# The counted groups' products in fp32 instead of three bf16 parts, with the counts widened on ScalarE

## The chip, the core and the metric

The kernel runs on one core of one Trainium2 chip. The metric is the device time of one execution in microseconds. A core has five engines with instruction streams of their own: TensorE (PE, with its weight loads as PEld), VectorE (DVE), ScalarE (ACT), GpSimd (POOL) and SyncE (SP). They wait for each other by semaphores. SP's stream here holds nothing but DMA issues; POOL's holds the gathers.

## The reference

Two layers of a graph network, a last product, and a normalized residual, on 12500 nodes of 256 features with 200000 edges sorted by `dst`:

```python
def _sage_conv(x, src, dst, W_l, b_l, W_r):
    msgs = x[src]
    agg = jax.ops.segment_sum(msgs, dst, num_segments=N_NODES)
    deg = jax.ops.segment_sum(jnp.ones((src.shape[0],), x.dtype), dst, num_segments=N_NODES)
    mean = agg / jnp.maximum(deg, 1.0)[:, None]
    return mean @ W_l + b_l + x @ W_r
h = relu(_sage_conv(x, src, dst, W1_l, b1, W1_r))
h = relu(_sage_conv(h, src, dst, W2_l, b2, W2_r))
out = layernorm(x + h @ W3 + b3)
```

`dst` is 12500 times the square of a uniform number, so low nodes have many edges and high nodes few. Everything is fp32.

## The kernel before

Nodes are handled in 98 blocks of 128, edges in 1563 tiles of 128. A node's sum over its edges is formed in one of two ways.

**Counted groups.** The hot nodes, those with many edges, come in groups of 256. For a group, `count` (L724) builds a matrix of counts, how often each source row occurs for each of the group's nodes: for every tile of edges DVE makes one-hot tables `pick`, `low` and `aft` (L738 to L746), PE multiplies them into `count_ps` (L765, L776, L780), and ACT writes the result to `counts` in bf16 (L782). `product` (L681) then multiplies the whole table of rows by the counts: for each of the 98 blocks of rows, PE accumulates rows times counts in PSUM (`dense_ps`, L707). So that these products are exact in bf16, the fp32 rows are split beforehand in three bf16 parts whose sum they are (`exact`, L656): those of `x` in the first stage (`split_rows`, L668, stored in `x3_d`), those of `h` when each block of the first layer is done (L976, stored in `h3_d`). A block of rows takes 3 parts x 2 halves of the features, six products of 128x256. Layer 1 counts five groups. Layer 2 uses eight: four whose counts layer 1 has stored in `count_d` and that are streamed back (`beside`, with sums in `beside_ps`) and four that are counted or kept; each of its four stages makes products for two groups at once, twelve for a block of rows. `degrees` (L791) sums a group's counts by 980 products of one column in all, to have the nodes' degrees on the partitions (`rdeg`).

**Gathers.** The edges of the other nodes are gathered: a round is four indirect DMAs of 128 rows from POOL into one of four buffers `got` (L262), then PE sums the rows by a one-hot `one` that DVE makes two rounds ahead (L274, four strips of 32 columns), ACT copies the result (`some`, L284), and one step later PE spreads it over the nodes (L290) and DVE adds it to `sums`, a ring of 8 blocks (L304). Layer 1 has 269 rounds, layer 2 has 235. A gather into a buffer waits until PE has summed what was in it.

**Blocks.** When all edges of a block are summed, `first_block` (L954) or `last_block` (L980) makes its output: rows are loaded and transposed on PE (L902), copied by ACT (L904), multiplied by both weights (`sage`: L925 for the sums, L930 for the own rows), combined on DVE (L936, L937) with the reciprocal degree as a scale for each partition, and passed through relu on ACT (L939). The last block transposes its result `h` once more, multiplies by `W3` (L997) and normalizes. A block is a generator; each `yield` ends a piece.

**The order.** The orders of PE and POOL are those in which the program is written (`manual_schedule`, L459). `layer` (L602) goes through the rounds and cuts each in three turns. In a turn it runs at most one piece of at most two open blocks (`MOST`), a block's next piece being due two turns after the last (`APART`), and fills up with counting and dense products: `mixed` (L815) interleaves a stage's parts in proportion to costs that the code states (`COST_DENSE` 0.7 for six products, `COST_DEGREES`, `count_cost`), and each round gets an equal share of the layer's sum of costs. In the third turn the sums of the round before (`summed`) come ahead of the piece. The loads of rows go through SP in the order of the program; four buffers of two blocks each hold them (`NROWS`, L692).

Of the kernel before, what the change touches and what calls it, by code (L numbers as in the profile page):

```python
# [23 lines left out]
P = 128  # L24
# [23 lines left out]
def by_runs(  # L48
# [82 lines left out]
    x3_d = dram.tile([P, NB, 3, D], BF16, name="x3_d")  # L131
    h3_d = dram.tile([P, NB, 3, D], BF16, name="h3_d")
# [8 lines left out]
    place = consts.tile([1, len(groups)], I32, name="place")  # L141
# [7 lines left out]
    offs = [consts.tile([1, n], I32, name=f"offs{g}") for g, n in enumerate(tiles_of)]  # L149
# [34 lines left out]
    rdeg = early.tile([P, NB], F32, name="rdeg")  # L184

    part_pool = ctx.enter_context(tc.tile_pool(name="part_ps", bufs=1, space=PSUM))
    mixed_pool = ctx.enter_context(tc.tile_pool(name="mixed_ps", bufs=2, space=PSUM))
# [3 lines left out]
    NROWS = 4  # L191
# [42 lines left out]
    class Gathers:  # L234
# [20 lines left out]
        def gathered(self, i):  # L255
# [13 lines left out]
            if r == 0:  # L269
                self.part_ps = part_pool.tile([P, D + 1], F32, name="part_ps")  # L270
            part_ps, width = self.part_ps, self.width

            for j in reversed(range(G)):
                strip = nc.tensor.matmul(part_ps[j * W:(j + 1) * W, :width], lhsT=one[:, j],  # L274
# [9 lines left out]
            nc.scalar.copy(some[:, :width], part_ps[:, :width])  # L284
# [289 lines left out]
    biases = consts.tile([P, 3, D], F32, name="biases")  # L574
    for i, b in enumerate((b1, b2, b3)):
        nc.scalar.dma_start(biases[:, i], b[None, :].to_broadcast([P, D]))
    zero = consts.tile([P, 1], F32, name="zero")
# [8 lines left out]
    split = keep.tile([P, 2, 3, D], BF16, name="split")  # L586
# [13 lines left out]
    MOST, APART = 2, 2  # L600

    def layer(gathers, block, n_pieces, dense, dense_cost, left):  # L602
# [5 lines left out]
        def begin():  # L608
            if waiting and len(queue) < MOST:
                b, *of = waiting.pop(0)  # L610
                p = block(b, *of)
                next(p)
                queue.append([b, p, n_pieces - 1, turn + APART])

        def pieces():
# [5 lines left out]
            if q:  # L621
                next(q[1])
                q[2:] = q[2] - 1, turn + APART
                if q[2] == 0:
                    done.add(q[0])
                    queue.remove(q)
# [12 lines left out]
        for i in range(i0, n + 1):  # L639
# [3 lines left out]
            for part in range(3):  # L643
                if part == 2 and before:
# [4 lines left out]
                pieces()  # L649
# [6 lines left out]
    def exact(t, s, rest):  # L656


        def upper(a):
            return a.bitcast(BF16).rearrange("p (n h) -> p n h", h=2)[:, :, 1]  # L660
# [5 lines left out]
        return leaves  # L666

    def split_rows(b):  # L668
        t = load_rows(x, N, b, "split_sb")
        s = split[:, b % 2]  # L670
        leaves = exact(t, s, work.tile([P, D], F32, name="rest", tag="own"))
        if b < 3:
            later(leaves)
        nc.sync.dma_start(x3_d[:, b], s)

# [5 lines left out]
    def product(table3, g, c_sb, beside=None):  # L681
# [6 lines left out]
        for t in ps:  # L688
            nc.tensor.matmul(t, lhsT=zeros_b, rhs=c_sb[:, :NC, :DN], start=True, stop=False)
        for b in range(NB):  # L690
            if b % 2 == 0:
                rows = work.tile([P, 2, 3, D], BF16, name="rows", bufs=NROWS)  # L692
                loads = [(nc.sync.dma_start(rows, table3[:, b:b + 2]), NROWS)]
                if beside is not None:
                    stream = streams[n_streamed % STREAMS]
                    n_streamed += 1
# [702 lines left out]
```

## Time and profile before

| what | value |
|---|---|
| three runs | 3265.1, 3281.22 (median), 3290.72 us |
| profiled execution | 3281.46 us, span 3279.7 us, mean granted TensorE clock 0.888 |
| PE busy | 2574.5 us (79%) |
| DVE, ACT, POOL busy | 1566.5 (48%), 1151.6 (35%), 1967.7 us (60%) |
| products of counted groups (L707) | 5292 `dense_ps` and 2352 `beside_ps`, 282 ns recorded each |
| split of rows on DVE (L662, L663), four groups of 98 | 40.5, 39.9, 41.1, 40.8 us |
| split of rows on ACT (L664, L665), four groups of 98 | 39.5, 39.0, 39.6, 39.7 us |
| evictions of counts on ACT (L782) | 688, 611.3 us |
| DMA | 612.56 MB, mean 187 GB/s |
| loads of split rows | 441 of 384 KB |
| PE idle before L925, on `sums` / before L902 on `h` | 69.7 and 85.0 / 51.4 us |

The first product of a counted group starts at 478 us (L689), the first of layer 2's at 1761 us. A group of instructions is read as: line, engine, operation, output<-inputs, shape, count, busy time, mean of one in ns, and the idle time of the engine just before them with what ended it. The recorded duration of a product overlaps with the next one's, so a product's cost is read from one start to the next.

### The profile page before, as it was taken

How to read it: one execution, taken by the hardware profiler on the slowest of the kernel's cores; microseconds unless marked ns; L12 is line 12 of the kernel's file. 1: busy time of each engine (PE TensorE's matmuls, PEld its weight loads, DVE VectorE, ACT ScalarE, POOL GpSimd, SP SyncE). 2: the span in 40 equal slices, each digit the busy share in tenths (PEclk: the TensorE clock that was granted, in tenths of full speed). 3: DMA queues.
4: the chain of work that ended last, by engine and by line, in shares of the span. 5: the costliest groups of instructions: out<-in, count | busy, mean ns of one | idle time of the engine just before them, and what ended most of it. 6: DMA issues, size and time to landing. Idle time of an engine off the chain costs nothing.

```text
span 3279.7 us, 56146 instructions
## 1 busy us (share of the span) xinstructions
PE 2574.5 (79%) x18946; PEld 1733.1 (53%) x18946; DVE 1566.5 (48%) x5560; ACT 1151.6 (35%) x2331; POOL 1967.7 (60%) x2026
## 2 busy tenths in 40 slices
PE   4565668878878878889865887878889888888876
PEld 2122335545546656656643555556556666666654
DVE  6778675544445555555552122334345444343334
ACT  0423664444444444455441001223233333221122
POOL 6665666666665656666664666565666666556652
PEclk9766679979979989989987899989989999999998
DMA  5565668658658758647644566565556656566642
GB/s 123 164 185 171 179 205 274 209 159 262 209 156 289 225 174 266 221 144 238 222 142 122 181 183 184 176 181 166 177 167 192 184 170 183 164 200 198 204 139 84
DMA packets 375242, 612.56 MB, mean 187 GB/s; under 512 B 72111, under 2 KB 253989, under 8 KB 374949
## 3 DMA queue, kind: packets, MB, share of 16 engines
q1 hardware_dynamic: 273235, 343.33, 34.0%
q0 software_dynamic: 96768, 264.37, 26.7%
q8 instruction: 155, 2.54, 0.3%
q10 hardware_dynamic: 4946, 1.19, 0.2%
q14 instruction: 138, 1.13, 0.1%
HBM read 518.75 MB, written 89.92 MB: 186 GB/s over the span
## 4 chain that ended last, share of the span: by engine, by line
PE 59%; issue 8%; another core or an unknown queue 7%; DVE 5%; ACT 3%; DMA 3%; POOL 0%; ACTq 0%; DVEq 0%; SPq 0%; POOLq 0%
PE dense_ps L707 16%; PE part_ps L274 7%; PE count_ps L776 7%; PE beside_ps L707 6%; PE block_ps L925 6%; PE block_ps L930 5%; PE sum_ps L290 4%; PE block_ps L997 3%; PE block_ps L902 3%; DMA rows<-x_d 2%; ACT counts L782 2%; PE count_ps L780 1%; PE sum_ps L296 1%; PE dense_ps L797 1%
## 5 line engine op out<-in xcount | busy, mean ns | idle before, releaser
L262 POOL DMA_INDIRECT got<-in_x_dram,src_t x1076 | 1067.8, 992 | 649.6 <-issue 258.2
L262 POOL DMA_INDIRECT got<-h_d,src_t x940 | 897.7, 955 | 617.1 <-issue 230.8
L707 PE MATMUL dense_ps<-counts,rows 128*128 128x256 bf16 x5292 | 981.6, 282 | 58.9 <-issue 31.5
L707 PEld LDWEIGHTS <-rows 128*128 128x128 bf16 x7644 | 745.2, 101 | 327.6 <-issue 165.6
L782 ACT CAST counts<-count_ps 128x882 f32 (+3 forms) x688 | 611.3, 888 | 533.1 <-PE count_ps L776 135.6
L707 PE MATMUL beside_ps<-spare,rows 128*128 128x256 bf16 x2352 | 570.3, 282 | 24.2 <-issue 23.2
L776 PE MATMUL count_ps<-pick,low 128*128 128x490 bf16 (+2 forms) x1188 | 378.7, 371 | 145.0 <-ACT counts L782 64.3
L274 PE MATMUL part_ps<-got,one 128*32 128x257 f32 (+1 forms) x4032 | 385.4, 434 | 53.2 <-issue 21.7
L738 DVE TENSOR_SCALAR pick<-steps,key_t 128x686 bf16<-128x686 f16 (+3 forms) x816 | 332.6, 410 | 117.6 <-remote 32.1
L218 DVE TENSOR_TENSOR one<-lo_t,lane_b 128x128 f32<-128x128 bf16 x504 | 144.1, 286 | 470.7 <-remote 150.1
L284 ACT COPY some<-part_ps 128x257 f32<-128x257 f32 (+1 forms) x355 | 132.8, 374 | 643.4 <-remote 293.7
L741 DVE TENSOR_SCALAR low<-lanes,low_t 128x130 bf16<-128x130 f16 x816 | 221.0, 272 | 212.4 <-remote 72.5
L304 DVE TENSOR_TENSOR sums<-sums,sum_ps 128x256 f32 x355 | 145.6, 410 | 250.2 <-remote 110.6
L290 PE MATMUL sum_ps<-two,some 128*128 128x128 f32 x1420 | 241.1, 296 | 13.1 <-issue 8.3
L290 PEld LDWEIGHTS sum_ps<-two,some 128*128 128x128 f32 x1420 | 211.2, 207 | 32.2 <-issue 19.3
L776 PEld LDWEIGHTS <-low 128*128 128x128 bf16 x1188 | 121.1, 103 | 181.9 <-issue 62.7
L936 DVE TENSOR_TENSOR own<-block_ps,biases 128x256 f32<-128x256 f32 x196 | 82.4, 420 | 220.3 <-PE block_ps L930 106.5
L274 PEld LDWEIGHTS part_ps<-got,one 128*32 128x32 f32 x4032 | 89.1, 113 | 184.1 <-issue 161.1
L925 PE MATMUL block_ps<-w1l_sb,sums 128*128 128x256 f32 x352 | 123.5, 483 | 69.7 <-issue 31.5
L933 ACT COPY sums<-zero 128x256 f32<-128x256 f32 x170 | 68.7, 404 | 306.0 <-PE block_ps L930 142.6
L904 ACT COPY own_t<-block_ps 128x256 f32<-128x256 f32 x294 | 109.3, 375 | 183.4 <-remote 65.4
L746 DVE TENSOR_SCALAR aft<-steps,after_t 128x98 bf16<-128x98 f16 x689 | 173.6, 252 | 0.0
(184 smaller groups left out, 2678.7 us busy)
## 6 DMA issues: line engine op xcount, KB each, us to landing
rows<-x_d SPq DMA_DIRECT2D x245, 384.0 KB
rows<-h_d SPq DMA_DIRECT2D x196, 384.0 KB
count_d<-counts SPq DMA_DIRECT2D x28, 896.0 KB
spare<-count_d SPq DMA_DIRECT2D x196, 128.0 KB
x_sb<-in_x_dram SPq DMA_DIRECT2D x194, 128.0 KB
x_d<-split SPq DMA_DIRECT2D x98, 192.0 KB
h_d<-split SPq DMA_DIRECT2D x98, 192.0 KB
got<-in_x_dram,src_t POOLq DMA_INDIRECT x1076
```

Of the source, the lines that this page charges most:

```text
L262: rows = nc.gpsimd.indirect_dma_start(out=g[:, j, :D], out_offset=None, in_=self.table, in_offset=bass.IndirectOffsetOnAxis(ap=src_t[:, e: ...
L274: strip = nc.tensor.matmul(part_ps[j * W:(j + 1) * W, :width], lhsT=one[:, j], rhs=g[:, j, :width], start=r == 0, stop=r == n - 1)
L290: nc.tensor.matmul(sum_ps[:, c], lhsT=some[:, c * P:(c + 1) * P], rhs=two, start=True, stop=True)
L304: nc.vector.tensor_add(own, own, sum_ps[:, :NC])
L707: nc.tensor.matmul(t[:, c], lhsT=rows[:, b % 2, k, c * P:(c + 1) * P], rhs=d, start=False, stop=b == NB - 1 and k == 2 and c == NC - 1)
L738: nc.vector.tensor_scalar(r[:, :w * NB], steps[:, :w * NB], key_t[g][:, t - lo_g:t - lo_g + 1], None, op0=OP.is_equal)
L741: nc.vector.tensor_scalar(low.rearrange("p (a b) -> p a b", a=5), lanes_5[:, :, :LW // 5], low_t[:, t:t + 1], None, op0=OP.is_equal)
L746: nc.vector.tensor_scalar(aft.rearrange("p (a b) -> p a b", a=7), steps_7[:, :, :NB // 7], after_t[g][:, t - after_from[g]:t - after_from[ ...
L776: nc.tensor.matmul(c[:, a * NB:b * NB], lhsT=s, rhs=r[:, a * NB:b * NB], start=True, stop=alone)
L782: nc.scalar.copy(to[:, :, bass.ds(off_act.at(t), w)], c.rearrange("p (d s) -> p s d", s=NB))
L925: product = nc.tensor.matmul(ps[:, 0], lhsT=agg[:, c], rhs=wl[:, c], start=c == 0, stop=c == NC - 1)
L930: product = nc.tensor.matmul(ps[:, 1], lhsT=own_t[:, c], rhs=wr[:, c], start=c == 0, stop=c == NC - 1)
```

## The change

Rows stay fp32 and are not split: `exact`, `split_rows`, the stage's `splits`, `x3_d` and `h3_d` go. `product` loads pairs of row blocks straight from `x` or `h_d`, and ACT copies each block of the counts, and of the streamed counts, to fp32 ahead of its products (`widen`, up to `NWIDE` = 8 buffers: six blocks ahead with one group, two with two). A block of rows then takes two fp32 products for a group instead of six bf16 ones, and `COST_DENSE` is 0.45 instead of 0.7. The degrees are summed on one partition by 98 products of 256 columns for a group and stored to `deg_d`; every first block reads its column from there, as a reciprocal. Pieces say how many turns later the next is due: two after the first, four after the others. A piece runs ahead of `summed` in its turn. The last block computes `h` transposed, so that the second transpose goes, and reads the reciprocal degrees as a row spread over the partitions. In layer 2 the gathers' sums alternate between two halves of a PSUM bank. The lists of offsets share one tile.

```diff
-    MOST, APART = 2, 2
+    MOST, SOON, APART = 2, 2, 4
...
             for part in range(3):
+                pieces()
                 if part == 2 and before:
                     gathers.summed(*before, done)
...
-                pieces()
                 fill(spent + (due - spent) / (3 - part))
...
-    def exact(t, s, rest):
-        leaves = nc.vector.tensor_tensor(rest, t, upper(t), op=OP.subtract)
-        nc.vector.tensor_tensor(s[:, 2], rest, upper(rest), op=OP.subtract)
-        nc.scalar.copy(s[:, 0], upper(t))
-        nc.scalar.copy(s[:, 1], upper(rest))
...
+        def pair(b):
+            rows = work.tile([P, 2, D], F32, name="rows", bufs=NROWS)
+            loads = [(load, NROWS) for load in load_pair(table, rows, b)]
+            stream = None
+            if beside is not None:
+                stream = streams[n_streamed % STREAMS]
+                n_streamed += 1
+                loads.append((nc.sync.dma_start(stream, count_d[beside, :, b:b + 2]), STREAMS))
...
+        def widen(b):
+            of = [c_sb[:, b, :DN]]
+            if beside is not None:
+                of.append(pairs[b - b % 2][1][:, b % 2])
+            widened[b] = []
+            for counted in of:
+                wide = work.tile([P, DN], F32, name="wide", bufs=NWIDE)
+                nc.scalar.copy(wide, counted)
+                widened[b].append(wide)
+
+        ahead = (NWIDE - 1) // len(ps) - 1
         for b in range(NB):
...
-            for k in range(3):
-                for c in range(NC):
-                    for t, d in zip(ps, counted):
-                        nc.tensor.matmul(t[:, c], lhsT=rows[:, b % 2, k, c * P:(c + 1) * P], rhs=d,
-                                         start=False, stop=b == NB - 1 and k == 2 and c == NC - 1)
+            for u in range(b, min(b + ahead + 1, NB)):
+                if u - u % 2 not in pairs:
+                    pair(u - u % 2)
+                if u not in widened:
+                    widen(u)
+            rows, _ = pairs[b - b % 2]
+            for c in range(NC):
+                for t, d in zip(ps, widened[b]):
+                    nc.tensor.matmul(t[:, c], lhsT=rows[:, b % 2, c * P:(c + 1) * P], rhs=d,
+                                     start=False, stop=b == NB - 1 and c == NC - 1)
...
-        for j in range(DN // P):
-            for b in range(NB):
-                nc.tensor.matmul(ps[:, 0, j:j + 1], lhsT=c_sb[:, b, j * P:(j + 1) * P], rhs=ones_b,
-                                 start=b == 0, stop=b == NB - 1)
+        for b in range(NB):
+            nc.tensor.matmul(ps[0:1, 0], lhsT=ones_b, rhs=c_sb[:, b, :DN], start=b == 0, stop=b == NB - 1)
...
-    COST_DENSE, COST_DEGREES, COST_SPLIT = 0.7, 1.6, 0.8
+    COST_DENSE, COST_DEGREES = 0.45, 1.6
...
     def first_block(b, agg=None):
...
-        yield True
+        yield SOON
+        deg = work.tile([P, 1], F32, name="deg")
+            nc.sync.dma_start(deg, deg_d[b, :, None])
+        x_t, copied = transposed(x_sb, turned(), "own_t")
+        yield APART
...
-        s = split[:, b % 2]
-        exact(h, s, own)
-        nc.sync.dma_start(h3_d[:, b], s)
-        yield True
+        yield APART
...
     def last_block(b, agg=None):
...
-        h2, _ = sage(h_t, copied, b, agg, of_ring, w2l_sb, w2r_sb, biases[:, 1], "h")
+        for side, (t, w) in enumerate(((agg, w2l_sb), (h_t, w2r_sb))):
+            for o in range(NC):
+                for c in range(NC):
+                    product = nc.tensor.matmul(ps[:, side, o * P:(o + 1) * P], lhsT=w[:, c, o * P:(o + 1) * P],
+                                               rhs=t[:, c], start=c == 0, stop=c == NC - 1)
...
+        for c in range(NC):
+            nc.scalar.activation(h2_t[:, c], own[:, c], AF.Relu, bias=b2_t[:, c:c + 1])
...
-        h2_t, _ = transposed(h2, turned(), "own_t")
```

More of the change, by code (lines that the diff above doesn't have):

```diff
@@ L832, in stored, with dense @@
             yield 0.5
[L834 removed]
+    def dense(table, waiting, with_deg, g, c_sb, beside=None):
         made = []
[L836 removed]
+        for p in product(table, g, c_sb, beside):
             if isinstance(p, float):
```

199 lines of the change are left out of this document (94 added, 105 removed).

## The prediction

> **What bounds the kernel now.** I read the page's busy line and chain first, then the matrix products one by one in the timeline, then busy time by stretches of 200 us, and last the groups of instructions by shape. The sum is made against the profiled execution: 3281.46 us, span 3279.7, 0.24 us above the median of the three runs (3265.1 to 3290.72).
>
> ```profile
> PE 2574.5 (79%) x18946; PEld 1733.1 (53%) x18946; DVE 1566.5 (48%) x5560; ACT 1151.6 (35%) x2331; POOL 1967.7 (60%) x2026
> PE 59%; issue 8%; another core or an unknown queue 7%; DVE 5%; ACT 3%; DMA 3%; POOL 0%; ACTq 0%; DVEq 0%; SPq 0%; POOLq 0%
> ```
>
> PE carries the chain; the other 41% are waits, handoffs and other engines. A timeline of PE shows what a product costs. Starts count, not durations, since one product overlaps the next:
>
> ```profile
> 2609.28 0.27 PE L707 MATMUL beside_ps<-spare,rows 128*128 128x256 bf16 x1
> 2609.39 0.27 PE L707 MATMUL dense_ps<-counts,rows 128*128 128x256 bf16 x1
> 2609.49 0.27 PE L707 MATMUL beside_ps<-spare,rows 128*128 128x256 bf16 x1
> 2609.60 1.03 PE L925 MATMUL block_ps<-w2l_sb,sums 128*128 128x256 f32 x4
> 2610.47 1.03 PE L930 MATMUL block_ps<-w2r_sb,own_t 128*128 128x256 f32 x4
> 2611.33 0.37 PE L776 MATMUL count_ps<-pick,low 128*128 128x490 bf16 x1
> ```
>
> A bf16 product over 256 columns takes 0.109 us from start to start. An fp32 one is two instructions (the two products of L930 in each block show as x4), and four instructions take 0.87 us: 0.2165 us an instruction, 0.433 a product.
>
> By stretches, the columns are PE busy, PEld, DVE, ACT, POOL, granted clock, DMA share, GB/s:
>
> ```profile
> 200.00:400.00 200.00, 120.95 (x591) 51.66 (x592) 150.38 (x518) 89.19 (x218) 125.77 (x124) 0.64 0.62 181
> 600.00:800.00 200.00, 159.66 (x1301) 104.82 (x1300) 93.86 (x373) 86.92 (x155) 123.36 (x127) 0.87 0.68 214
> 1400.00:1600.00 200.00, 174.65 (x1407) 122.18 (x1406) 110.03 (x410) 100.45 (x188) 123.98 (x126) 0.91 0.62 194
> 1800.00:2000.00 200.00, 160.16 (x1170) 107.54 (x1171) 37.61 (x114) 18.21 (x48) 124.21 (x131) 0.89 0.59 180
> 2800.00:3000.00 200.00, 174.82 (x1384) 133.39 (x1377) 80.65 (x246) 47.95 (x124) 115.89 (x122) 0.98 0.62 189
> ```
>
> POOL's count is the progress of the gathers. It stays at 122 to 131 in 200 us although PE is busy between 121 and 175. So the pace hardly follows the amount of PE work; handoffs between engines hold it, until PE is as full as in the last row, where it falls to 122. These handoffs show as idle time ahead of the blocks' products:
>
> ```profile
> L925 PE MATMUL block_ps<-w1l_sb,sums 128*128 128x256 f32 x352 | 123.5, 483 | 69.7 <-issue 31.5 <-DVE sums L304 17.5 <-DVE deg L969 7.8
> L925 PE MATMUL block_ps<-w2l_sb,sums 128*128 128x256 f32 x328 | 105.1, 449 | 85.0 <-ACT own_t L904 26.9 <-DVE own L937 18.2 <-DVE sums L304 17.7
> L902 PE MATMUL block_ps<-ident,h 128*128 128x128 f32 x196 | 42.8, 302 | 51.4 <-ACT h L939 34.6 <-issue 14.4 <-ACT own_t L904 1.2
> L797 PE MATMUL dense_ps<-ones_b,counts 128*128 128x1 bf16 x980 | 40.2, 165 | 25.1 <-issue 18.2 <-ACT d_sb L716 6.4 <-DMA h_d<-split 0.5
> ```
>
> **The products.** 7644 bf16 products (5292 dense and 2352 beside) at 0.1092 us are 835 us of PE. They become 13 x 98 x 2 = 2548 fp32 products at 0.433, 1103 us: +268. The degrees' 980 one-column products start every 0.025 us (24.5 us); 490 of 256 columns at 0.109 take 53: +29. The transposes of h2 go: 196 at 0.11, -21.5. PE's own work grows by 276, 132 in layer 1 and 144 in layer 2. The bounds of what reaches the end are 0 (the pace stays at its 122 to 131) and all 276.
>
> I place it by stretch. Layer 1's 132 us add about 20 to each 200. Six stretches from 400 to 1600 have PE busy 154, 160, 162, 170, 171 and 175; up to 175 the pace did not suffer, and what would lie above it is 0, 5, 7, 15, 16 and 20: 63 us. In layer 2 the stretches before 2800 hold 642 gathers at 1.558 us; at the 1.639 of the last row they cost +52. The last dense stage is beyond any row: the planner's weights (0.7 to 0.45 a product group) give it 46 rounds of four gathers instead of 50, so 170 us of dense products fall on them instead of 128, and I count its 41 us whole. Half of the transposes' 21 comes off. Sum: 63 + 52 + 41 - 11 = +145, nearer to the middle than to an end.
>
> **The blocks.** Pieces of a block stand four turns apart instead of two, run ahead of the gathers' sums in their turn, and the transpose of h2 with its wait on ScalarE is gone. Idle before L925 was 69.7 + 85.0 + 16 (its groups on d_sb and split), before L902's h 51.4, before L797 25.1: 247 us. None of it gone, or all of it, are the ends. I take 60%, -150: four turns are more than a round of 6.3 us, and the waits named (DVE sums, ACT own_t, ACT h) are each under 8 us long. What then comes late is the last product of a block; two blocks in ten turns are 1.67 rounds a block, and by the code's bounds on the sorted edges at most one comes in two rounds. The degree's column now waits for a stored reciprocal; its load has four turns before its use, and the 29.5 us that DVE idled for it lose their cause.
>
> **The first stage.** The splits of x leave: 98 x 2 instructions on DVE at 0.41, the same on ACT at 0.405, 98 loads and 98 stores. Before 430 us DVE is busy 150 of 200, and PE's products there wait 42.2 us for DVE's low, 20.6 for ACT's evictions, 16 for other DVE work. I take -55 of these 79; with POOL's 1.25 us from gather to gather as the least, the floor of 55 rounds is 275 us against 370, so the ends are 0 and -95. In layer 1's blocks the splits of h go as well, 98 x 2 on each engine: hidden, since ACT and DVE idle there, and a help to the handoffs above if not.
>
> **Widening.** 1274 copies of 128x256 on ACT; the nearest rows are the plain copies of that size at 0.375 to 0.405 us: 516 us. ACT loses 158 of splits and 37 of h2's copies and rises from 1152 to about 1500, 46%. It is not full, but in order: a widening stands behind evictions and activations that wait for PE, and these wait behind it. It is made six blocks ahead in layer 1 and two in layer 2, about 5.2 and 3.5 us of products alone. Ends: 0, and the 64.3 us that PE waits for 688 evictions, 0.093 each, on all 1274: +119. I take +20, near the low end, for the start of each of nine groups, where the copies stand behind the last evictions.
>
> **Queues and bytes.** SP loses 294 transfers and gains about 115 (rows of degrees, columns of the dense blocks). Loads of rows shrink from 384 to 256 KB, 441 times, and 51 MB of splitting go: 109 of 612.56 MB. The packets become 1024 bytes instead of 3072; the trace's packets of these sizes took 50 and 164 ns on average, the same per byte, so nothing is charged. POOL's instructions are unchanged. The 26.3 us that products waited for rows are the most that could be won.
>
> Sum: 145 - 150 - 55 + 20 = -40, from 3281 to 3241 us.
>
> **Rivals.** *PE full* (slower). If PE's own queue sets the pace, all 276 land, and half of the 150 at the blocks only moves to the next wait: 3281 + 276 - 75 - 55 + 20 = 3447. For it: PE is 59% of the chain, and 2800:3000 is slower at 175. Against: 1400:1600 is as busy at 126 gathers. It decides once the rounds outside the last stage exceed 6.4 us. *ScalarE late* (slower): PE stands before the products for a widened block, +119 in place of +20, 3340. For it: ACT already idles in order behind PE's results; against: the lead of two to six blocks. *Handoffs free* (faster): the pace follows POOL, which issues every 1.25 us where it need not wait (2616.25, 2617.50, 2618.76 in its timeline) against 1.56 now. If a third of that gap closes over 1950 gathers, -200: 3080. With it comes the clock: from 400 to 3000 the granted clock averages 0.905 and was 0.98 in the densest stretch; at 0.98 the PE work there (products by their starts: some 1900 us now, 2176 with the 276) would take 184 less. The Trainium skill, "TensorE: Matmul & The Clock Gate", section "What's actually happening", has the clock halved after an idle window and released by sustained activity. By that rule the denser stream alone brings the 184 us, and the sum by it would be 3057; the trace agrees in the sign (0.64 where PE is busy 121 of 200, 0.98 at 175), but 0.91 at 174.65 shows that density alone does not settle it. *The products are cheap*: were an fp32 product one instruction, 552 us instead of 835; L930's count, two for each product, excludes it but for a few per cent.
>
> **Chances.** Forecast, 3150 to 3320: 0.45, of which 0.25 lies more than 1% below. PE full 0.22, ScalarE late 0.13 (0.02 within 1%), handoffs free 0.18, cheap products 0.02. One per cent, 33 us, is about what a measurement can tell here. Faster by more: 0.25 + 0.18 + 0.02 = 0.45. Within: 0.18 + 0.02 = 0.20. Slower: 0.02 + 0.22 + 0.11 = 0.35. The range leaves out the outer part of both sides: 3060 to 3450.
>
> **What would show it.** Dense products at 0.433 us each and PE work up by 276: sure, or the sum is void. Idle before the blocks' first product under 100 us. First dense product before 430 us, not 478. POOL's gathers in 200 us: 124 to 130 in layer 1, about 120 from the third quarter on. ACT's widening at 0.4 us, with little idle on PE named after it. Wrong would be: under 118 gathers in all stretches (PE full), over 140 (handoffs free), or PE waiting for the widened blocks by more than 60 us.

## The result, and the profile after

| | before | after |
|---|---|---|
| median of four runs | 3273.7 us (3265.1 to 3290.72) | 3319.49 us (3299.49 to 3326.19) |
| profiled execution | 3281.46, span 3279.7 | 3320.8, span 3319.0 |
| granted clock | 0.888 | 0.921 |
| DMA | 612.56 MB | 509.24 MB |

The ratio is 1.0111, 95% interval 1.0081 to 1.0141: slower by 1.1%, where 1.2% faster had been forecast. The time lies inside the forecast range. The runs fell on chips of two kinds, on which the kernel before takes 3274 to 3295 us (the runs above; e9 to e17, on three chips) or 2743 to 2748 us (e1 to e8, all on one chip); each kernel is compared with the kernel before on its own chip. They are called the late and the prompt chip below, for a reason that the first experiments show.

The page's busy line and the chain by engine, of the changed kernel:

```profile
PE 2746.4 (83%) x16496; PEld 1958.1 (59%) x16496; DVE 1512.5 (46%) x5172; ACT 1455.6 (44%) x3213; POOL 1957.1 (59%) x2026
PE 75%; another core or an unknown queue 8%; DVE 6%; issue 6%; ACT 3%; POOL 1%; DVEq 1%; DMA 0%; ACTq 0%; SPq 0%; POOLq 0%
```

PE is busy 172 us longer, and its share of the chain went from 59 to 75%. The groups by shape that answer to those shown of before (L726 was L707; L960 and L993 were L925; L1011 was L997; L810 was L797; the last line is the widening):

```profile
L726 PE MATMUL dense_ps<-wide,rows 128*128 128x256 f32 x3528 | 1005.4, 395 | 10.7 <-issue 5.0 <-ACT wide L713 3.0 <-ACT counts L796 1.1
L960 PE MATMUL block_ps<-w1l_sb,sums 128*128 128x256 f32 x352 | 116.6, 461 | 102.0 <-DVE sums L312 74.0 <-DVE spare L949 12.0 <-DVE spare L308 7.7
L993 PE MATMUL block_ps<-sums,w2l_sb 128*128 128x128 f32 x656 | 109.5, 318 | 97.8 <-DVE sums L312 37.3 <-ACT some L292 18.7 <-ACT wide L713 17.1
L993 PE MATMUL block_ps<-d_sb,w2l_sb 128*128 128x128 f32 x128 | 20.5, 311 | 10.9 <-DVE own L1002 6.0 <-issue 3.8 <-DVE z L1013 1.1
L1011 PE MATMUL block_ps<-w_sb,h 128*128 128x256 f32 x392 | 108.1, 400 | 35.4 <-ACT h L1005 29.9 <-issue 4.9 <-ACT wide L713 0.6
L810 PE MATMUL dense_ps<-counts,ones_b 128*1 128x256 bf16 x490 | 63.0, 279 | 8.1 <-issue 3.4 <-ACT d_sb L735 2.8 <-ACT h L974 1.9
L713 ACT CAST wide<-counts 128x256 f32<-128x256 bf16 x882 | 349.8, 406 | 423.7 <-PE dense_ps L726 173.0 <-PE part_ps L282 52.4 <-remote 44.2
```

The number after the last bar is what the change was to win. Ahead of the blocks' products and the degrees PE now idles 102.0 + 97.8 + 10.9 + 35.4 + 8.1 = 254 us. Before it was 69.7 + 85.0 + 15.9 + 51.4 + 25.1, and 11.6 ahead of the last product: 259.

```profile
L997 PE MATMUL block_ps<-w_sb,own_t 128*128 128x256 f32 x392 | 107.9, 399 | 11.6 <-ACT some L284 3.5 <-DVE own L937 2.4 <-DVE z L999 2.2
```

The wait ahead of the second transpose (51.4) went and that of the degrees shrank by 17; the wait ahead of the sums' products grew by 40 and that ahead of the last product by 24, nearly as much. By stretches (PE busy, PEld, DVE, ACT, POOL, granted clock, DMA share, GB/s):

```profile
200.00:400.00 200.00, 122.33 (x630) 54.98 (x629) 124.98 (x444) 71.55 (x126) 123.19 (x128) 0.69 0.33 95
600.00:800.00 200.00, 159.39 (x997) 109.08 (x996) 92.51 (x332) 97.93 (x195) 119.17 (x126) 0.91 0.59 174
1400.00:1600.00 200.00, 182.31 (x1131) 127.95 (x1129) 109.51 (x370) 113.42 (x234) 124.05 (x125) 0.97 0.52 152
2400.00:2600.00 200.00, 171.75 (x1061) 131.94 (x1060) 78.78 (x265) 89.17 (x202) 112.81 (x119) 0.95 0.52 154
```

POOL's gathers per 200 us, 126 and 125 in the two rows of layer 1, hardly moved there (127 and 126 before); from 1800 to 3000 us they are 119 to 129. From the start of one dense group's first product to the next (the first figure is that of the first one), and from the last to the end:

| us | first | layer 1 | layer 2 | end |
|---|---|---|---|---|
| before, late chip | 478 | 247, 249, 229, 255, 303 | 316, 384, 383 | 436 |
| after, late chip | 440 | 258, 267, 240, 248, 306 | 304, 409, 417 | 430 |
| before, prompt chip (e5) | 443 | 205, 204, 193, 207, 258 | 253, 305, 310 | 370 |
| after, prompt chip (e6) | 370 | 205, 206, 209, 223, 280 | 243, 332, 358 | 401 |

On the chip of the result the first stage gives 38 us, layer 1 takes 36 back and layer 2 with the end 41.

### The profile page after: what moved, and what is told of

The parts are those of the page before. It is cut to its first block, busy times and chain, and to the rows that moved or that the text cites. A ratio compares the mean times of both kernels' runs of the same rounds, so it can differ in the third digit from the quotient of the medians.

```text
span 3319.0 us, 51820 instructions
## 1 busy us (share of the span) xinstructions
PE 2746.4 (83%) x16496; PEld 1958.1 (59%) x16496; DVE 1512.5 (46%) x5172; ACT 1455.6 (44%) x3213; POOL 1957.1 (59%) x2026
## 2 busy tenths in 40 slices
DMA packets 404928, 509.24 MB, mean 153 GB/s; under 512 B 70748, under 2 KB 340135, under 8 KB 404647
## 3 DMA queue, kind: packets, MB, share of 16 engines
q10 hardware_dynamic: 5074, 1.06, 0.2%
## 4 chain that ended last, share of the span: by engine, by line
PE 75%; another core or an unknown queue 8%; DVE 6%; issue 6%; ACT 3%; POOL 1%; DVEq 1%; DMA 0%; ACTq 0%; SPq 0%; POOLq 0%
PE dense_ps L726 24%; PE beside_ps L726 10%; PE part_ps L282 8%; PE count_ps L790 7%; PE block_ps L993 7%; PE sum_ps L298 5%; PE block_ps L960 3%; PE block_ps L965 3%; PE block_ps L1011 3%; ACT counts L796 2%; PE dense_ps L810 1%; PE block_ps L908 1%; POOL got L270 1%; PE count_ps L794 1%
## 5 line engine op out<-in xcount | busy, mean ns | idle before, releaser
L726 PE MATMUL dense_ps<-wide,rows 128*128 128x256 f32 x3528 | 1005.4, 395 | 10.7 <-issue 5.0
L726 PEld LDWEIGHTS dense_ps<-wide,rows 128*128 128x128 f32 x3528 | 634.4, 194 | 168.4 <-issue 90.9
L713 ACT CAST wide<-counts 128x256 f32<-128x256 bf16 x882 | 349.8, 406 | 423.7 <-PE dense_ps L726 173.0
L726 PE MATMUL beside_ps<-wide,rows 128*128 128x256 f32 x1568 | 475.7, 385 | 5.7 <-issue 5.4
L790 PE MATMUL count_ps<-pick,low 128*128 128x490 bf16 (+2 forms) x1188 | 361.2, 359 | 110.0 <-ACT counts L796 65.4
L282 PE MATMUL part_ps<-got,one 128*32 128x257 f32 (+1 forms) x4032 | 360.6, 420 | 56.1 <-ACT some L292 20.7
L726 PEld LDWEIGHTS beside_ps<-wide,rows 128*128 128x128 f32 x1568 | 304.3, 194 | 52.8 <-issue 9.7
L298 PEld LDWEIGHTS sum_ps<-two,some 128*128 128x128 f32 x1420 | 215.8, 206 | 47.3 <-issue 15.9
L960 PE MATMUL block_ps<-w1l_sb,sums 128*128 128x256 f32 x352 | 116.6, 461 | 102.0 <-DVE sums L312 74.0
L282 PEld LDWEIGHTS part_ps<-got,one 128*32 128x32 f32 x4032 | 87.1, 112 | 187.3 <-issue 139.3
L993 PE MATMUL block_ps<-sums,w2l_sb 128*128 128x128 f32 x656 | 109.5, 318 | 97.8 <-DVE sums L312 37.3
```

Source lines behind the costliest of these rows:

```text
L282: strip = nc.tensor.matmul(part_ps[j * W:(j + 1) * W], lhsT=one[:, j], rhs=g[:, j, :width], start=r == 0, stop=r == n - 1)
L298: nc.tensor.matmul(sum_ps[:, c], lhsT=some[:, c * P:(c + 1) * P], rhs=two, start=True, stop=True)
L713: nc.scalar.copy(wide, counted)
L726: nc.tensor.matmul(t[:, c], lhsT=rows[:, b % 2, c * P:(c + 1) * P], rhs=d, start=False, stop=b == NB - 1 and c == NC - 1)
L790: nc.tensor.matmul(c[:, a * NB:b * NB], lhsT=s, rhs=r[:, a * NB:b * NB], start=True, stop=alone)
L960: product = nc.tensor.matmul(ps[:, 0], lhsT=agg[:, c], rhs=w1l_sb[:, c], start=c == 0, stop=c == NC - 1)
```

## The experiments

**The two chips: e5, e6.** Both kernels unchanged.

> The kernel before, unchanged, for a profile from the chip of these runs, where it takes 2743 us against 3274 in the runs of the result. Theory A (what differs is how late PE's signals arrive): VectorE and ScalarE see a signal of PE within 0.05 us of its instruction's end, not 0.5 to 1 us later, gathers go in runs of a dozen or more at 1.25 us, and PE's work is the same 0.109 us a product. Rival (another clock or slower transfers): the granted clock or the durations of gathers and copies differ by 15 per cent.

> The changed kernel, unchanged, beside the kernel before on one chip. If this is a chip where PE's signals arrive at once, theory A (PE is then the bound, and fp32 products cost most of their 276 us): 2860 to 2900 us, ratio 1.04 to 1.06, as with the products alone (1.049). Rival (the blocks' rework and the products help each other): under 2840. If it is a chip with late signals: 1.01 again.

Measured: before 2747.57 us, after 2826.24, ratio 1.0279 (1.0261 to 1.0298). The granted clock differs by 5% (0.934 against 0.888) and the durations hardly: a gather occupies POOL for 0.95 us in the median on both, an fp32 product takes 0.216 us an instruction on both. What differs is when PE's signals arrive. For every PE instruction that raises a semaphore I took the time from its modelled end to the semaphore's next recorded change. Given while POOL is in a run of gathers, it is 0.47 us in the median for the changed kernel on the late chip, and over 2.5 for a tenth of them (0.97 and 3.2 for the kernel before); on the prompt chip 0.01, with 0.02 to 0.04 at the ninth tenth. On the late chip many changes of PE's semaphore come in a bunch: 695 of them 1.9 to 2.3 us after the start of the last gather of a run, which is 1 us after its end, and 38 in the half microsecond from 1.3 to 1.8 (a run here is gathers less than 1.35 us apart). Of the changes of VectorE's and ScalarE's semaphores 52 and 38 lie in the same 0.4 us.

The late chip's record of semaphore changes has gaps: 3205 changes for 4128 PE instructions of the changed kernel that raise the semaphore (2497 for 2892 before), against 4124 and 2890 on the prompt chip. Where a change is missing the next one was taken, so the times of the late chip are upper bounds. The waiting engines show the same without that record. Of the VectorE instructions that waited for PE's semaphore alone and had idled, 36% started more than 0.3 us after the end of the last PE instruction that raises it (57% for the kernel before), on the prompt chip 1 and 2%. Of the ScalarE instructions that waited for VectorE's alone, none did on either chip.

So there many of PE's signals, and hardly any of the other engines', are held while gathers run, and a bunch of them is let go when a run is over. Not all are held: 1289 of the 3205 changes are recorded inside runs. Whether POOL's issuing holds them or the transfers that it starts is not shown, since the gathers' packets end in the same stretch as the bunch, with a peak 2.0 to 2.4 us after the last gather's start. A timeline of the changed kernel on the late chip shows one such hold (the lines between are left out):

```profile
1187.69 0.95 POOL L270 DMA_INDIRECT got<-in_x_dram,src_t  x1 [0.30 <-issue]
1188.62 0.22 PE L304 MATMUL sum_ps<-two,some 128*1 128x128 bf16 x1
1189.30 0.64 PE L282 MATMUL part_ps<-got,one 128*32 128x257 f32 x8
1192.43 0.28 DVE L755 TENSOR_SCALAR low<-lanes,low_t 128x130 bf16<-128x130 f16 x1 [4.31 <-remote]
1193.81 0.40 DVE L752 TENSOR_SCALAR pick<-steps,key_t 128x686 bf16<-128x686 f16 x1 [0.93 <-remote]
1193.94 1.08 POOL L270 DMA_INDIRECT got<-in_x_dram,src_t  x1 [0.30 <-issue]
1196.66 0.28 DVE L308 TENSOR_TENSOR spare<-spare,sum_ps 1x128 f32 x1 [2.45 <-remote]
1196.87 0.40 DVE L312 TENSOR_TENSOR sums<-sums,sum_ps 128x256 f32 x1
1197.42 1.19 PE L960 MATMUL block_ps<-w1l_sb,sums 128*128 128x256 f32 x2 [7.48 <-DVE sums L312]
```

PE ended `sum_ps` at 1188.84. VectorE adds it at 1196.66, when gathers that began before 1187.69 and ended at 1195.02 are through; PE, whose next instruction is the block's product, stands for 7.48 us. Two waits of VectorE ahead of that, 4.31 and 0.93 us, ended inside the run. "remote" is what the profile writes where it finds no writer that ended shortly before the signal came. The Trainium skill, "Perfetto Trace Analysis", section "Per-engine timelines", has PE's signal pushed when PSUM has acknowledged the bytes, after an end that the profile only estimates; on the prompt chip the trace agrees (0.01 us), and nothing on that page would hold it for 8 us.

Without the hold the kernel before comes near POOL's floor. On the prompt chip two of its stretches are:

```profile
600.00:800.00 200.00, 172.88 (x1514) 120.88 (x1514) 111.83 (x432) 102.72 (x185) 149.55 (x155) 0.93 0.80 253
1800.00:2000.00 200.00, 185.96 (x1539) 138.55 (x1536) 95.21 (x325) 73.94 (x131) 151.04 (x158) 0.98 0.72 218
```

These are 155 and 158 gathers, near the 160 that 1.25 us each allow, and PE waits 12.2 us each ahead of the two L925 groups where it was 69.7 and 85.0. Theory A of e5 holds but for the runs of a dozen gathers or more: with up to 1.6 us from start to start counted as one run, half have six or fewer. Expected of e6 was 1.04 to 1.06; the rival (rework and products help each other, under 2840 us) is right there.

**Is it the gathers: e9, e10.** In both kernels half of the gathers are left out; the strips still sum four slots.

```diff
-            for j in range(G):
+            for j in range(0, G, 2):
                 e = t0 + j * n + r - C0 * P
...
-            nc.vector.memset(g[:, :, D:D + 1], 1.0)
+            nc.vector.memset(g, 1.0)
```

> The kernel before with half of the gathers left out (two of the four of a round; the strips still sum all four slots). POOL then needs 2.5 us a round instead of 5.0. Theory (where PE's signals come at once, POOL's 1.25 us a gather is the floor under the kernel before: its rounds take 5.01 to 5.39 us in seven of eight dense stages): 2540 to 2640 us. Rival (PE or the handoffs hold it, and POOL only follows): 2700 us or more. If the chip has late signals: PE's signals are held for 2.5 us and not for 5, and the kernel gains 300 us or more on 3274.

> The changed kernel with the same half of the gathers left out. Theory (PE, 92 per cent busy, is the bound of the changed kernel, POOL only of its first stages and the first of layer 2): 2730 to 2790 us, so that the two kernels without POOL's floor lie about 190 us apart instead of 79, as the 276 us of products less the 73 of the first stage would have it. Rival (POOL bounds both): both fall alike and stay 80 apart.

These fell on a late chip (before 3294.95 us). Measured: 2602.36 us, ratio 0.7911 (0.7891 to 0.7932), and 2766.27 us, 0.8406 (0.8385 to 0.8427). Half the gathers take 693 us from the kernel before, more than the 547 that lie between the chips, and PE becomes the bound of both, as the busy lines show, e9's and then e10's:

```profile
PE 2328.0 (90%) x18946; PEld 1642.6 (63%) x18946; DVE 1562.9 (60%) x5560; ACT 1159.0 (45%) x2331; POOL 999.8 (38%) x1018
```

```profile
PE 2572.7 (93%) x16496; PEld 1862.6 (67%) x16496; DVE 1506.9 (55%) x5172; ACT 1494.5 (54%) x3213; POOL 996.8 (36%) x1018
```

The gain is beyond the 300 us that e9 named for a late chip, and e10 is inside its range. So the gathers, by their issuing or their transfers, and not PE's work set the 6.2 to 6.4 us of a round on the late chip. The two kernels are then 164 us apart; with the first dense product at 332 instead of 419 us, the later stages cost 251 us more, nearly the whole 276 of added PE work. Where PE is busy 90% and more, the products cost nearly what their starts say.

**The parts alone: e1, e2 (prompt), e11, e12 (late).** e1 and e11 are the changed kernel with the old products:

```diff
-            rows, _ = pairs[b - b % 2]
-            for c in range(NC):
-                for t, d in zip(ps, widened[b]):
...
+            for k in range(3):
+                for c in range(NC):
+                    for t, d in zip(ps, counted):
+                        nc.tensor.matmul(t[:, c], lhsT=rows[:, b % 2, k, c * P:(c + 1) * P], rhs=d,
...
-    COST_DENSE, COST_DEGREES = 0.45, 1.6
+    COST_DENSE, COST_DEGREES, COST_SPLIT = 0.7, 1.6, 0.8
```

e2 and e12 are the kernel before with the new `product`, `widen`, `COST_DENSE` 0.45 and no splits; its `sage`, its degrees and `APART` 2 stay (the lists of offsets share one tile, for room).

> The changed kernel with the bf16 products, the splits and COST_DENSE 0.7 of the kernel before: of the change only the blocks' turns, the degrees, the transposed h2 and the alternating halves are left. Theory A (the reworked blocks bring next to nothing, since PE's signals reach VectorE and ScalarE late while POOL issues gathers, wherever a block's piece stands): 3255 to 3285 us, as the kernel before, with the first dense product at about 478 us again and the blocks' first products waiting some 170 to 200 us. Rival B (the blocks gave the forecast 150 us and the fp32 products took them back): 3120 to 3180 us.

> The kernel before with nothing but the fp32 products, the widening, COST_DENSE 0.45 and the shorter first stage. Theory A: about 3310 to 3330 us, the whole loss of the change, since 38 us of first stage are won and some 80 us lost to the products. Rival B: 3400 us or more, since the products would cost 190 and nothing pays for them.

> Once more the blocks' rework alone, with bf16 products, for a chip on which PE's signals come late. Theory (the waits ahead of a block's first product are signals held while POOL issues, so another place for the piece moves them and does not end them): within 1 per cent of the kernel before, ratio 0.99 to 1.01, with 150 us or more of idle time ahead of the blocks' first products. Rival (the rework gives its 150 us there): 0.95 to 0.96. On a chip with prompt signals it would be 1.006 again.

> Once more the fp32 products and the shorter first stage alone, for a chip with late signals. Theory (rounds of 6.2 us hide most of the added PE work; 38 us come off the first stage): ratio 1.01 to 1.025. Rival (the products cost what the forecast's blocks paid for): 1.05 or more. On a chip with prompt signals it would be 1.049 again.

| ratio to before | late chip | prompt chip |
|---|---|---|
| blocks' rework alone | 1.0067 (1.0036 to 1.0099) | 1.0056 (1.0035 to 1.0078) |
| products and first stage alone | 0.9984 (0.9959 to 1.0009) | 1.0488 (1.0456 to 1.0521) |
| both | 1.0111 (1.0081 to 1.0141) | 1.0279 (1.0261 to 1.0298) |

The microseconds expected of e1 to e4 were written for a late chip; there e11 is as its own theory has it (within 1%, with 245 us of idle time ahead of the blocks' first products, in the two groups below and one on `d_sb`), and e12 is under what either theory wrote.

```profile
L960 PE MATMUL block_ps<-w1l_sb,sums 128*128 128x256 f32 x352 | 124.3, 486 | 105.8 <-DVE sums L314 58.3 <-issue 16.9 <-DVE spare L310 16.7
L996 PE MATMUL block_ps<-sums,w2l_sb 128*128 128x128 f32 x656 | 114.1, 327 | 129.3 <-DVE sums L314 63.2 <-ACT some L294 37.9 <-issue 16.6
```

The rework wins nothing by itself on either chip: on the prompt one there is little to win above POOL's floor, on the late one it costs 22 us (12 to 32 by its interval). Beside fp32 products it wins 2% on the prompt chip, where PE is busy 92% in e6, and loses 1.3% on the late one (1.0111 less 0.9984), by runs of two chips with some 0.4% of uncertainty. The products alone are even on the late chip: their first dense product starts at 435 us, 43 earlier, so the added work and the widening cost some 38 us after it.

**The price of PE's work and of widening: e3 (prompt), e13 (late), e4, e7 (prompt).** e3 and e13 leave out a quarter of the products (276 us of PE), e4 the widening, e7 widens two blocks in one copy.

```diff
                 for t, d in zip(ps, widened[b]):
+                    if b % 2 and c == 0:
+                        continue
```

```diff
             for counted in of:
-                wide = work.tile([P, DN], F32, name="wide", bufs=NWIDE)
-                nc.scalar.copy(wide, counted)
-                widened[b].append(wide)
+                widened[b].append(same)
```

```diff
-            of = [c_sb[:, b, :DN]]
+            of = [c_sb[:, b:b + 2, :DN]]
...
-                wide = work.tile([P, DN], F32, name="wide", bufs=NWIDE)
+                wide = work.tile([P, 2, DN], F32, name="wide", bufs=NWIDE // 2)
```

> The changed kernel with a quarter of the fp32 products left out (the first half of the features in every second block of rows): 276 us less work for PE, with all the widening, loads and gathers kept. Theory A (a round of gathers waits on late signals and PE's work is only partly on the path, some 30 per cent): 3220 to 3260 us, with 125 to 130 gathers in 200 us. Rival C (PE is full): 3040 to 3080 us. Rival D (the pace does not depend on PE's work at all): 3305 to 3330 us.

> Once more the changed kernel with a quarter of the fp32 products left out, 276 us less work for PE, for a chip with late signals. If a round there waits mostly on signals, 60 to 100 us come off the changed kernel: ratio 0.98 to 0.99 to the kernel before. If PE's work counted whole: 0.925. If it did not count: 1.01. On a chip with prompt signals it would be 0.977 again.

> The changed kernel with the widening left out: the products read one constant fp32 tile, so ScalarE does 1274 copies (508 us) less and PE signals no released buffers; PE's work is the same. If the widening is hidden but for a group's start, as forecast (20 us): 3290 to 3310 us. If ScalarE's lateness sets the pace (119 us): about 3200 us. If the released buffers' signals stand ahead of more urgent ones: 3230 to 3270 us.

> The changed kernel with one widening copy for two blocks of rows: half as many copies on ScalarE and half as many signals of released buffers from PE, the products the same. Theory (widening is hidden, its count of signals too): within 0.5 per cent of the changed kernel. Rival (ScalarE's in-order queue is late for the products): 30 to 60 us less than the changed kernel.

Measured: e3 0.9773 (0.9746 to 0.9799), 5.1% under the changed kernel's 1.0279, some 139 of the 276 us; e13 0.996 (0.9939 to 0.9981), 1.5% under 1.0111, some 50 us. So PE's work counts about half on the prompt chip and under a fifth on the late one; neither "full" nor "not at all" holds, and on the late chip it counts less than the theory of e13 had it. e4 1.0322 (1.0293 to 1.0351) and e7 1.0292 (1.0275 to 1.031): 508 us less of ScalarE, or half its copies, bring nothing. Widening is hidden on the prompt chip. On the late one it was not taken away. There `wide` is named for 3.0 us ahead of the dense products that read it; the 17.1 and 0.6 us named ahead of L993 and L1011 are ahead of products that read no widened block.

**The turns: e14, e15 (late).** In the order of PE's instructions of the changed kernel, the first product with the sums comes directly behind a round's strips (L282) for 85 of 98 first blocks and 68 of 98 last blocks: its piece falls in the first turn of a round. In the kernel before it was 87 and 52, with 69 and 74 us of the idle time: the four turns left most of these products where they had been. e14 sets the pieces two turns apart, e15 also puts the last product four turns after the weights':

```diff
-    MOST, SOON, APART = 2, 2, 4
+    MOST, SOON, APART = 2, 2, 2
```

```diff
-    MOST, SOON, APART = 2, 2, 4
+    MOST, SOON, APART, LATE = 2, 2, 2, 4
...
         x_sb = load_rows(x, N, b, "x_sb")
-        yield APART
+        yield LATE
         nc.vector.tensor_add(x_sb, x_sb, biases[:, 1])
```

> The changed kernel with its pieces two turns apart again (SOON and APART 2), and nothing else. Theory (the spacing has no part in the time: what the rework saves beside fp32 products is the transposes, the copies and the waits that it leaves out): within 0.5 per cent of the changed kernel. Rival (four turns give the products of a block their operands in time): 1 per cent or more slower than the changed kernel.

> The changed kernel with the first pieces two turns apart, as in e14, and the last product of a block four turns after its weights' products. Theory (a piece that comes right behind the strips of a round, in the first turn of three, meets every held signal whole; in e14 that is the last product, 85 times of 98, with 101 us of idle time ahead of it): the wait ahead of the last product falls under 50 us and the wait ahead of the weights' products stays near 73; on a chip with late signals 3215 to 3250 us, ratio 0.98 to 0.99. Rival (the wait only moves on to the next reader): 0.995 as e14. On a chip with prompt signals 1.02 to 1.03.

Measured: e14 3265.55 us, ratio 0.9951 (0.9925 to 0.9978), and e15 3229.0 us, 0.9835 (0.9799 to 0.987). My theory for e14, that the spacing has no part, fell: its own rival had named the spacing, but with the wrong sign, since two turns beat four by 1.6%. The groups of e14:

```profile
L960 PE MATMUL block_ps<-w1l_sb,sums 128*128 128x256 f32 x352 | 107.7, 434 | 45.1 <-DVE sums L312 21.0 <-ACT own_t L910 7.5 <-issue 6.9
L993 PE MATMUL block_ps<-sums,w2l_sb 128*128 128x128 f32 x656 | 92.8, 286 | 28.1 <-ACT own_t L910 14.7 <-issue 5.5 <-DVE own L1002 3.1
L1011 PE MATMUL block_ps<-w_sb,h 128*128 128x256 f32 x392 | 128.9, 458 | 100.7 <-ACT h L1005 83.8 <-DVE own L1002 11.5 <-issue 2.8
```

The products with the sums come behind strips 6 and 9 times now, and their wait falls from 200 to 73 us; the last product (L1011) comes there 85 times and waits 100.7. The groups of e15:

```profile
L960 PE MATMUL block_ps<-w1l_sb,sums 128*128 128x256 f32 x352 | 109.6, 440 | 39.1 <-DVE sums L312 18.8 <-ACT own_t L910 10.9 <-issue 5.6
L993 PE MATMUL block_ps<-sums,w2l_sb 128*128 128x128 f32 x656 | 98.9, 299 | 55.0 <-ACT own_t L910 24.8 <-DVE own L1002 11.0 <-DVE sums L312 8.7
L993 PE MATMUL block_ps<-d_sb,w2l_sb 128*128 128x128 f32 x128 | 17.8, 282 | 6.1 <-DVE own L1000 3.2 <-DVE sums L312 1.7 <-ACT wide L713 1.2
L1011 PE MATMUL block_ps<-w_sb,h 128*128 128x256 f32 x392 | 108.1, 399 | 12.4 <-DVE own L1002 6.1 <-ACT h L1005 2.5 <-DVE z L1013 2.0
```

The last product's wait is under 50 us as expected, that of the sums' products at 94 instead of 73. The idle time ahead of all these and of the degrees (9.1) is 122 us instead of 254, and the kernel is 90 us shorter: the turn in which a piece stands is worth more than the whole forecast. The place alone does not decide: 33 last products still come directly behind strips in e15, four turns after their weights' products, and wait 4.4 us in all. It beats both kernels on the late chip; on the prompt one it was not run.

**Other versions: e8 (prompt), e16, e17 (late).** e8 is the kernel before with fp32 products for the first counted group alone, so that the splits leave the first stage (`EARLY` is 56); e16 is e11 with e15's turns; e17 is e15 with the own rows' products first and the reciprocal on a column.

```diff
-            if g == 0:
-                parts.append((splits(), NB * COST_SPLIT))
-            else:
...
+            if g == 1:
+                parts.append((splits(0, EARLY), EARLY * COST_SPLIT))
+            if g == 2:
+                parts.append((splits(EARLY, NB), (NB - EARLY) * COST_SPLIT / 0.55))
```

```diff
-            nc.vector.tensor_scalar(deg_row, deg_row, 1.0, None, op0=OP.max)
-            nc.vector.reciprocal(deg_row, deg_row)
...
+            nc.vector.tensor_scalar(deg, deg, 1.0, None, op0=OP.max)
+            nc.vector.reciprocal(deg, deg)
...
+                nc.sync.dma_start(deg_d[b, :, None], deg)
...
-        for side, (t, w) in enumerate(((agg, w2l_sb), (h_t, w2r_sb))):
+        for side, t, w in ((1, h_t, w2r_sb), (0, agg, w2l_sb)):
```

> The kernel before, with fp32 products from x for the first counted group alone, so that no split is needed before it: 56 of the 98 splits run beside the first group's products, 42 beside the second's. PE gains 21 us of work. Theory (the splits lengthen the first stage by 86 us where signals come at once, as the start of the first dense product shows, 452 against 364 to 369 us, and elsewhere they hide): 2690 to 2715 us against 2743, ratio 0.98 to 0.99. Rival (VectorE, over 60 per cent busy in the next stages, gives the time back there): 2735 to 2760.

> The same turns with the bf16 products, the splits and COST_DENSE 0.7 of the kernel before (e11 with other turns). Theory as in e15: on a chip with late signals 40 to 80 us less than e11, ratio 0.98 to 0.995; whether it is under e15 tells whether the fp32 products are worth their shorter first stage. On a chip with prompt signals 0.995 to 1.005, since POOL's floor holds it there.

> e15 with the own rows' products ahead of the sums' products in both kinds of blocks, and with the reciprocal degree taken on a column of 128 partitions (0.157 us before) and stored back, and not on a row of one partition (0.933 us). Theory (both give the sums' signals a microsecond more): 5 to 20 us less than e15. Rival (neither is on the path): as e15 within 0.3 per cent.

Measured: e8 1.0008 (0.9993 to 1.0022). Its first dense product starts at 348 us instead of 443, and the next two stages take 237 and 242 instead of 205 and 204: three quarters come back at once, the rival's case. e16 1.0022 (1.0001 to 1.0043), less than expected: the turns help the bf16 kernel by 0.5% only, so beside these turns the fp32 version is 1.9% the shorter on the late chip. The idle time ahead of the blocks' products and the degrees falls in e16 as it did in e15, from 287 us in e11 to 156, but the time follows by 15 us only: the two groups of dense products idle 129 us instead of 64. Idle time at one place is not time won. The two groups in e16:

```profile
L718 PE MATMUL dense_ps<-counts,rows 128*128 128x256 bf16 x5292 | 1001.0, 284 | 86.0 <-issue 64.0 <-DMA rows<-x_d 20.0 <-DMA got<-h_d,src_t 0.5
L718 PE MATMUL beside_ps<-spare,rows 128*128 128x256 bf16 x2352 | 577.6, 284 | 43.4 <-issue 42.4 <-remote 0.2
```

e17 1.0291 (1.0253 to 1.033), a miss on both theories. Its group of dense products shows a part:

```profile
L726 PE MATMUL dense_ps<-wide,rows 128*128 128x256 f32 x3528 | 1027.0, 401 | 53.9 <-DMA rows<-in_x_dram 41.2 <-issue 11.0 <-ACT wide L713 0.8
```

Rows, which cost no wait that the group names in e15, come late for 41.2 us, a quarter of the 156 us between e17 and e15. SP's queue, which holds the loads of rows too, waits 78.0 us at the new store of `deg` for the column's load and 20.9 for VectorE's reciprocal, and 127.3 at the column's load for the store of the row (13.8 in e15). That is read from the trace; the rest of the 156 us is not assigned, and the two edits of e17 were not taken apart.

## Why the prediction was wrong, point by point

**The blocks, -150 us: the step that failed.** It took 60% of 247 us of idle time as won because "four turns are more than a round of 6.3 us, and the waits named (DVE sums, ACT own_t, ACT h) are each under 8 us long". The rework cost 22 us alone and some 42 beside the products (1.0111 less 0.9984). Four turns after the second piece is the first turn of a round, directly behind the strips, where these products mostly stood before; there the product meets signals that can be held until a run of gathers is over. Idle time ahead of the sums' products grew from 171 to 211 us, where under 100 was named as the sign. The distance in turns was counted, the place in the round and what PE has to do between was not. With other turns (e15) the same rework is 1.5% better than the products alone, about 49 us, a third of the forecast. That the turns count is shown by e14 and e15, whose edits change nothing else, though place and distance change together there. That held signals are the reason rests on the traces and on e9, since no run takes the hold alone away.

**The products, +145: mis-sized.** The prices were right: 0.216 us an instruction from start to start, two for a product, and in e10 against e9 251 of 276 us land where PE is busy 90% and more. On the late chip little does: e12 leaves 38 us after the first stage, with the widening, and e13 gives 50 us for 276. The stretch-by-stretch sum read "up to 175 the pace did not suffer" as a limit of PE; busier stretches (182.31 with 125 gathers) keep the pace too.

**The first stage, -55:** 38 in the result, 43 in e12, 73 on the prompt chip. Right in sign and size; the first dense product at 440 us missed the mark of 430.

**Widening, +20:** the copy takes 0.406 us, as forecast. The 20 us are not shown: PE's dense products wait 3.0 us for it on the late chip, and on the prompt chip taking it away wins nothing (e4, e7).

**Queues and bytes, 0:** bytes fell by 103 MB and loads of rows no longer stand among the dense products' waits; no run separates their worth.

**The sum.** In place of 145 - 150 - 55 + 20 stand 38 with the widening, 42 and -43: +37, against 39 between the two spans. The 38 and the 42 are differences of the same measured times, so this sum closes by construction and is no check. That the time fell inside the forecast range is luck: the blocks missed by 192 us, and the products with the widening came out 127 us lower than forecast.

**The reading under it.** That PE's work does not hold the pace was right on the late chip (e9, e13). "Handoffs between engines hold it" fits the late signals in the traces, but the handoffs in turn follow the gathers: with half of them left out the kernel before takes 693 us less. That distance in turns alone would shorten the handoffs was wrong (e11).

**The rivals.** PE full: no; gathers stayed at 119 to 129 from 1800 us on, and e13 refutes it for the late chip; on the prompt one about half of it holds (e3). ScalarE late: not on the prompt chip (e4); on the late one no run took the widening away. Handoffs free: not by this change; it is what the prompt chip is like, where the kernel before takes 2747 us with 155 gathers in 200. The clock rule named there: the granted clock rose from 0.888 to 0.921 with PE denser, in the rule's direction, and brought no shorter time.

## What to carry to other kernels

More turns between a producer and its reader do not by themselves end the reader's wait; look at which instruction stands directly ahead of the waiting one, put work there, and count what returns in the time, since a wait can move on to the next reader (e16). Before a change moves work to the engine with the most busy time, leave out a known part of that engine's work: what returns (a fifth on one chip here, half on the other) is the price of adding. And compare on one chip: the same two kernels are 1.1% apart on one and 2.8% on the other.

## What the runs showed of the hardware

PE's signals can be held while gathers run: on the late chip 57% of VectorE's waits for PE alone in the kernel before ended more than 0.3 us after PE's last instruction that raises the semaphore, on the prompt one 2%. The same kernel takes 3274 us on one and 2747 on the other; of what was compared, only this and the granted clock (0.888 and 0.934) differ. That the hold makes the difference in time is not shown by a run that changes it alone, and why one chip holds them is open.

A reciprocal of 128 elements on one partition took 0.933 us, where 128 partitions of one element took 0.157 before:

```profile
L950 DVE RECIPROCAL spare<-spare 1x128 f32<-1x128 f32 x88 | 82.0, 933 | 0.5
```

The Trainium skill, "VectorE: DVE Perf Modes", section "First, the fixed hardware budget", has the reciprocal as an iterative divide with a repeat count of 8; the trace agrees in the direction: such a row takes over four times as long as the maximum with 1 on the same row, 0.220 us (L949).
